# A running-sum copy moved ahead of the seventh exp, and another order of loading at the start

## The chip, the core and the metric

The kernel runs on one core of a Trainium2 chip. The metric is the device time of one execution in microseconds (us). Engines are named as the profile names them: PE is the matrix engine, PEld its weight loads, DVE the vector engine, ACT the scalar engine, POOL the GpSimd engine, SP the engine that issues most of the transfers. ACTq, SPq and DVEq mean that engine's sequencer (issue and waiting), not its arithmetic.

## The reference

Two graph layers, each with a residual and a layer norm, on x of 128 batches with 128 tokens and 512 features, all in float32, with an adjacency mask of 128 x 128 for each batch:

```python
# layer 0: masked attention with 8 heads of 64, then a projection
q, k, v = x @ Wq + bq, x @ Wk + bk, x @ Wv + bv
attn = softmax(where(adj > 0, q @ k.T / sqrt(64), -1e9))     # per head
x = layernorm(x + relu((attn @ v) @ Wo + bo))
# layer 1: additive attention over the same mask
Wh = x @ W
e = leaky(s_i[:, :, None] + s_j[:, None, :])       # s_i, s_j: Wh @ a1, Wh @ a2
att = softmax(where(adj > 0, e, -9e15), axis=1)
x = layernorm(x + leaky(att @ Wh))
```

## The kernel before

**Products with seven multiplications.** The five big products (x by Wq, Wk and Wv; the attention output by Wo; the layer-1 input by W) are cut into 2 x 2 blocks and done with seven block multiplications instead of eight (`strassen`, L279). Each product is a list of seven steps, called p1, p5, p6, p2, p7, p4, p3 in that order. Three of them, p1, p6 and p7, multiply into one running sum in PSUM, the bank that the trace calls `p_y` or `st_y`. After p1 and again after p6 and p7, ACT copies the running sum out to SBUF (`t0`, `t2`, `t3`), because the next step adds to the same bank and the intermediate sums are needed later. So the matrix engine may start p7 only once ACT has finished the copy `t2` that follows p6. The block sums of the left operand (`left_blocks`, L268) are four POOL operations; those of the weights (`right_blocks`, L134) are four DVE operations.

**Two kinds of product.** `group_product` (L328) makes q, k and v for four batches at a time (a group). Its steps are handed out through `group()` calls. `pair_product` (L413) does the projections by Wo and W for two batches at a time (a pair). Its steps are handed out through `pair()` calls. The copy of a pair's running sum is `read_out` (L434, the copy is line L436, tile `pr_t`). In odd stages the pair is a projection by Wo (`project_o`), in even stages one by W (`project_w`).

**The main loop** (L767) has one stage for each batch t. All five engines run in the order written there (`manual_schedule`), with waits only for data and buffers. In each stage after the third, the program starts the logits of batch t (L469), adds the mask, takes the maxima, runs eight exps on ACT, one for each head (L490), then eight divisions on ACT (L504), writes the result to DRAM and reads it back in another layout (`spread`, L508), and DVE transposes it in the next stage (`transpose`, L517). Between these calls stand `group()` and `pair()`. Before the change, p6 of the pair is the third `pair()` of the stage, and it stands after the seventh exp:

```python
            sm.exp(4, 5)
            last.transpose()
            group()
            sm.reciprocals(0)
            sm.exp(6)
            fin.store()
            pair()
            sm.exp(7)
```

On PE nothing stands between these lines but the multiplications of `group()` and `pair()`, and on DVE nothing of `pair()`. p7 follows at the next-but-one `pair()`.

**The start.** SP loads the four batches of the first group (`x_rows`), then half of Wq, Wk, Wv. ACT issues the other half of Wq and the two biases. DVE reorders the features of each batch (L733), PE transposes them (L743), DVE or ACT copies them to `xT` (L744). DVE scales four blocks of Wq (L747) and makes the block sums of Wq (L137 to L140). POOL makes the block sums of x (L273 to L276). For the first group the Q steps go p1, p2, p5, p6, p7. p1 and p2 use the first two batches and the first two blocks of Wq alone (XS[0], XS[1] and the ACT-issued half of Wq); p5 onward use the block sums. `x_turns` (L713) tells at which stage the later batches are transposed, and so when their loads (`xz`, L240, four for each batch) are issued. The block sums of Wv are written to DRAM (`wv`, L168) and fetched back piece by piece (`wv_n`, L386) through a ring of three buffers.

Of the kernel before, what the change touches and what calls it, by code (L numbers as in the profile page):

```python
# [17 lines left out]
GROUP = 4  # L18
# [6 lines left out]
def kernel(  # L25
# [56 lines left out]
    nc = tc.nc  # L82
    B, P, D = x.shape
# [179 lines left out]

    def sum_x(g):
        sums = big.tile([P, 3, 2, 2 * P], F32, name="xS")
        XS[g] = left_blocks(XT[g], sums)

    def left_blocks(xT, sums):  # L268


        xt = xT.rearrange("p (i c) (h t) -> p i h c t", i=2, h=2)
        a11, a12, a21, a22 = (xt[:, i, h] for h in range(2) for i in range(2))
        nc.gpsimd.tensor_add(sums[:, 0], a21, a22)  # L273
        nc.gpsimd.tensor_sub(sums[:, 1], sums[:, 0], a11)
        nc.gpsimd.tensor_sub(sums[:, 2], a11, a21)
        nc.gpsimd.tensor_sub(a21, a12, sums[:, 1])  # L276
        return (a11, a12, a21, a22, sums[:, 0], sums[:, 1], sums[:, 2])

    def strassen(bank, multiply, read, add):  # L279

# [86 lines left out]
    def products(g):  # L367

        for h in range(2):
            Q[g, h] = big.tile([P, NC, HALF], F32, name="qT", bufs=4)  # L370
            K[g, h] = big.tile([P, NC, HALF], F32, name="kT", bufs=3)
            V[g, h] = big.tile([P, 2, D], F32, name="v", bufs=3)

        def features_first(dst):
            return lambda h, o: dst[g, h][:, 2 * o : 2 * o + 2, :]

        def tokens_first(dst):
            return lambda h, o: dst[g, h][:, :, o * HALF : (o + 1) * HALF]

        ring, todo = {}, [0, 4, 5, 1, 6, 3, 2]  # L380

        def fetch():
            if todo:
                n = todo.pop(0)
                ring[n] = work.tile([P, 2, HALF], F32, name="wv_n", bufs=3)
                nc.sync.dma_start(ring[n], wv[n])  # L386

        chains = [
            group_product(g, 3 * g, lambda n: wq[:, PLACE[n]], features_first(Q), True, b_cols[:, 0, :]),
            group_product(g, 3 * g + 1, lambda n: wk[:, PLACE[n]], features_first(K), True),  # L390
            group_product(g, 3 * g + 2, ring.pop, tokens_first(V), False),
        ]

        def with_fetch(step, n=1):
            def run():
                step()
                for _ in range(n):
                    fetch()

            return run  # L400

        chains[1][0] = with_fetch(chains[1][0], 2)
        chains[2][0] = with_fetch(chains[2][0])
        chains[1][5] = with_fetch(chains[1][5])
        for n in (1, 2, 3):
            chains[2][n] = with_fetch(chains[2][n])

        order = [chains[0][n] for n in ((0, 3, 1, 2, 4) if g == 0 else range(5))]
        order += [chains[1][0], *chains[0][5:], *chains[1][1:5]]
        order += [chains[2][0], chains[1][6], chains[1][5], *chains[2][1:5]]  # L410
        return order + chains[2][5:]
# [112 lines left out]
    def attend(sm):  # L524

        b = sm.b
        v = V[b // GROUP, b % GROUP // 2][:, b % 2, :]
        p = psum("p_oT").rearrange("p (c q) -> p c q", c=NC)
        for c in range(NC):
            for r in range(2):  # L530
                h = 2 * c + r
                nc.tensor.matmul(  # L532
                    p[r * HD : (r + 1) * HD, c, :],
                    v[:, h * HD : (h + 1) * HD],
                    sm.paT[:, r * NC + c, :],
                    start=True,
                    stop=True,
                )
        pair, h = divmod(b, 2)

        def copy():
            if h == 0:
                OT[pair] = work.tile([P, NC, 2 * P], F32, name="oT")
            for c in range(NC):
                nc.scalar.activation(  # L545
                    OT[pair][:, c, h * P : (h + 1) * P],
                    p[:, c, :],
                    AF.Identity,
                    bias=b_cols[:, 1, c : c + 1],
                )  # L550
            if h == 1:
                sums = work.tile([P, 3, 2, P], F32, name="oS")
                OT[pair] = left_blocks(OT[pair], sums)

        return copy

# [56 lines left out]
    def transpose_x1(b):  # L613
        pair, h = divmod(b, 2)
        if h == 0:
            X1T[pair] = work.tile([P, NC, 2 * P], F32, name="x1T")
        transpose_blocks(X1T[pair][:, :, h * P : (h + 1) * P], X.pop((b, 1)))
        if h == 1:
            sums = work.tile([P, 3, 2, P], F32, name="x1S")
            X1T[pair] = left_blocks(X1T[pair], sums)  # L620

    def project_w(pair):

# [87 lines left out]
    sm = fin = edge = none  # L711

    def x_turns(t):  # L713
        if t < -1:
            return () if t == -3 else (4, 5, 6)
        return [b for b in [(), (t + 7, t + 8), (t + 8,), (t + 8,)][t % GROUP] if on(b)]

    x_rows = [work.tile([P, 2, D], F32, name="x_rows", tag=tag) for tag in ("pa", "paz")]  # L720
    for b in range(GROUP):
        nc.sync.dma_start(x_rows[b // 2][:, b % 2, :], x[b])
    load_blocks(Wq, columns(wq), nc.scalar, only=0)
    nc.scalar.dma_start(b_rows[:NC, :], bq.rearrange("(c p) -> c p", p=P))
    nc.scalar.dma_start(b_rows[NC:, :], bv.rearrange("(c p) -> c p", p=P))
    load_blocks(Wq, columns(wq), nc.sync, only=1)
    load_blocks(Wk, columns(wk), nc.sync)
    XT[0] = big.tile([P, NC, GROUP * P], F32, name="xT")
# [1 line left out]
    def order_features(b):  # L730
        rows = x_rows[b // 2][:, b % 2, :]
        turned = work.tile([P, D], F32, name="x_turned", tag="xz", bufs=3)
        nc.vector.tensor_copy(  # L733
            turned.rearrange("p (c q i) -> p c q i", q=4, c=4),
            rows.rearrange("p (q c i) -> p c q i", q=4, c=4),
        )
        return turned

    def transpose_rows(b, turned, copy):

        p = psum("p_x").rearrange("p (c k) -> p c k", c=NC)
        for c in range(NC):
            nc.tensor.transpose(p[:, c, :], turned[:, c * P : (c + 1) * P], ident)  # L743
        copy(XT[0][:, :, b * P : (b + 1) * P], p)  # L744
# [5 lines left out]
    turned = [order_features(b) for b in range(2)]  # L750
    transpose_rows(0, turned[0], nc.vector.tensor_copy)
    transpose_rows(1, turned[1], nc.scalar.copy)
    turned.append(order_features(2))
    scale(0)
    transpose_rows(2, turned[2], nc.scalar.copy)
    turned.append(order_features(3))
    scale(1)
    transpose_rows(3, turned[3], nc.vector.tensor_copy)
    turn_biases()
    sum_x(0)  # L760
    scale(2)
    wq_sums[0]()
    scale(3)
    for op in wq_sums[1:]:
        op()
    chores += right_blocks(places(wk)) + load_wv()
    for t in range(-3, B + 9):  # L767
        pair_steps = []
# [30 lines left out]
        if t < 3:  # L799
            sm.maxima()  # L800
            group(2)
            if on(t - 2):
                load_residual(t - 2)
            if t == 0 and on(GROUP):
                sum_x(1)
            sm.exp(0, 1, 2, 3)
            last.transpose()
            group()
            sm.reciprocals(0)
            sm.exp(4, 5, 6, 7)  # L810
            sm.reciprocals(1)
            sm.divide(0, 1, 2)
            group()
            copy_o = attend(last) if last is not none else none.copy
            sm.divide(3, 4)
            copy_o()
            sm.divide(5, 6, 7)
            if on(t + 1):
                mask_float(t + 1)
        else:  # L820
            sm.maxima()
            group()
            edge = EdgeSoftmax(t - 7) if on(t - 7) else none
            fin.residual()
            if on(t - 2):
                load_residual(t - 2)
            edge.maxima()
            fin.stats()
            if t % GROUP == 0 and on(t + GROUP):
                sum_x(t // GROUP + 1)  # L830
            pair()
            sm.exp(0, 1, 2, 3)
            edge.exp()
            pair()
            sm.exp(4, 5)
            last.transpose()
            group()
            sm.reciprocals(0)
            sm.exp(6)
            fin.store()  # L840
            pair()
            sm.exp(7)
            edge.divide()
            pair()
            sm.reciprocals(1)
            sm.divide(0, 1, 2, 3)
            group()
            sm.divide(4, 5)
            pair()
            sm.divide(6, 7)  # L850
            if on(t + 1):
                mask_float(t + 1)
            copy_o = attend(last) if last is not none else none.copy
            if t % 2 == 0:
                copy_o()
            group()
# [56 lines left out]
```

## Time and profile before

| | before |
|---|---|
| time, median of 3 (lowest to highest) | 2514.77 us (2514.57 to 2516.88) |
| span of the profiled execution | 2513.0 us |
| PE busy | 2444.2 us, 97% |
| PEld busy | 2000.3 us, 80% |
| DVE busy | 1817.5 us, 72% |
| ACT busy | 1429.8 us, 57% |
| POOL busy | 781.1 us, 31% |
| granted PE clock, mean | 0.989 |
| DMA | 379.92 MB, 151 GB/s |

A busy share is an average over the whole span. Where the span has stages with different limits, it says little about any one of them, so the views by stretch of time and the waits of single instructions have to be read beside it. In timeline rows the columns are start, busy time, engine, line, operation, tiles out<-in, shapes and count, and in brackets how long the engine had been idle and what released it.

### The profile page before, as it was taken

The numbers are of one execution on the slowest core, as the hardware profiler recorded it, in microseconds if no ns is written. First come the engines' busy times: TensorE is split into PE (matmuls) and PEld (weight loads), VectorE is DVE, ScalarE is ACT, GpSimd is POOL, SyncE is SP. The second block draws the span as 40 slices with busy tenths as digits, with TensorE's granted clock in tenths as the row PEclk, the third lists the DMA queues.
The fourth block names the chain that finished last, engine by engine and source line by source line (L and its number), as shares of the span: only waits on it lengthen the run. The fifth ranks groups of instructions, "written<-read, shape, count | busy, mean of one in ns | idle before, by whom it ended". The sixth has DMA issues, their size and how long they took to land.

```text
span 2513.0 us, 43768 instructions
## 1 busy us (share of the span) xinstructions
PE 2444.2 (97%) x13713; PEld 2000.3 (80%) x13713; DVE 1817.5 (72%) x3758; ACT 1429.8 (57%) x5187; POOL 781.1 (31%) x1161
## 2 busy tenths in 40 slices
PE   8899999999999999999999999999999999999975
PEld 6688888888888888888888888888888888888853
DVE  5767777777776777776777776777777777777675
ACT  2565565565565565565565556556556556556551
POOL 2222323322323323323323323323323323333232
PEclk9999999999999999999999999999999999999987
DMA  6544444544444544544544544544544444544531
GB/s 186 180 144 142 160 159 138 172 151 143 159 150 149 168 151 143 167 144 152 164 149 147 164 144 152 167 145 151 165 142 153 161 147 152 167 147 143 164 119 47
DMA packets 351112, 379.92 MB, mean 151 GB/s; under 512 B 38936, under 2 KB 255008, under 8 KB 350880
## 3 DMA queue, kind: packets, MB, share of 16 engines
q1 hardware_dynamic: 350288, 376.59, 46.6%
q8 instruction: 110, 1.80, 0.3%
q14 instruction: 122, 1.00, 0.1%
q10 hardware_dynamic: 592, 0.53, 0.1%
HBM read 240.91 MB, written 136.05 MB: 150 GB/s over the span
## 4 chain that ended last, share of the span: by engine, by line
PE 92%; DVE 3%; DMA 2%; ACT 1%; issue 1%; SPq 1%; POOL 0%; DVEq 0%; POOLq 0%; ACTq 0%
PE st_y L345 26%; PE p_y L425 17%; PE st_w L345 13%; PE p_w L425 8%; PE st_x L345 7%; PE lg L469 5%; PE p_oT L532 5%; PE p_h L672 4%; PE p_x L425 4%; ACT pa L490 1%; PE p_e L643 1%; PE p_e L644 1%; DMA wv_n<-wv 0%; ACT pa L504 0%; DVE st L559 0%
## 5 line engine op out<-in xcount | busy, mean ns | idle before, releaser
L564 POOL TENSOR_SCALAR ve<-mv 128x1 f32<-128x1 f32 x256 | 68.7, 268 | 1372.9 <-DVE mv L561 1372.9
L490 ACT ACTIVATE pa<-pa,nmax 128x128 f32<-128x128 f32 x1024 | 399.9, 392 | 48.3 <-DVE nmax L484 33.8
L504 ACT ACTIVATE pa<-pa,rs 128x128 f32<-128x128 f32 x1024 | 336.4, 395 | 30.1 <-DVE rs L500 30.1
L545 ACT ACTIVATE oT<-p_oT,b_cols 128x128 f32<-128x128 f32 x512 | 145.6, 367 | 202.1 <-PE p_w L425 200.1
L478 DVE TENSOR_TENSOR pa<-lg,mf 128x512 f32<-128x512 f32 x256 | 164.5, 684 | 100.6 <-PE lg L469 98.1
L322 ACT COPY st_t<-st_y 128x512 f32<-128x512 f32 x192 | 110.7, 577 | 157.1 <-PE st_y L345 157.1
L469 PEld LDWEIGHTS lg<-kT,qT 64*128 64x128 f32 x2048 | 124.2, 187 | 93.7 <-issue 93.7
L490 ACT ACTIVATION_READ_ACCUMULATOR pa<-pa,nmax 128x1 f32 x1024 | 193.3, 189 | 0.0
L566 POOL TENSOR_TENSOR rstd<-ve,mhalf 128x1 f32<-128x1 f32 x256 | 176.8, 691 | 21.4
L436 ACT COPY pr_t<-p_y 128x256 f32<-128x256 f32 (+1 forms) x384 | 139.7, 364 | 59.8 <-PE p_y L425 53.2
L519 DVE STREAM_TRANSPOSE paT<-paz 128x1024 f32<-128x1024 f32 x128 | 159.3, 1245 | 1.0 <-issue 0.3
L484 DVE TENSOR_REDUCE nmax<-pa 128x8 f32<-128x1024 f32 x128 | 156.2, 1220 | 4.4
L326 ACT ACTIVATE st_t<-st_y,b_cols 128x256 f32<-128x256 f32 x192 | 80.7, 471 | 126.2 <-PE st_y L345 126.2
L672 PE MATMUL p_h<-wh,att 128*128 128x512 f32 x256 | 133.9, 605 | 17.6 <-DVE att L663 17.6
L632 DVE TENSOR_TENSOR wh<-p_w,pr_t 128x257 f32<-128x257 f32 x128 | 54.1, 423 | 133.1 <-PE p_w L425 83.1
L425 PE MATMUL p_y<-w,x1S 128*128 128x257 f32 x512 | 136.5, 389 | 12.9 <-ACT pr_t L436 10.7
L469 PE MATMUL lg<-kT,qT 64*128 64x128 f32 x2048 | 148.7, 285 | 0.0
L532 PEld LDWEIGHTS p_oT<-paT,v 128*64 128x64 f32 x2048 | 111.0, 138 | 47.0 <-issue 41.2
L532 PE MATMUL p_oT<-paT,v 128*64 128x128 f32 x2048 | 142.3, 282 | 3.6 <-DVE paT L519 3.6
L425 PE MATMUL p_y<-wo,oS 128*128 128x256 f32 x512 | 132.6, 382 | 7.9 <-ACT pr_t L436 7.9
L646 ACT ACTIVATE e<-p_e,wh 128x128 f32<-128x128 f32 x128 | 47.3, 369 | 161.0 <-PE p_e L644 161.0
L425 PE MATMUL p_y<-w,x1T 128*128 128x257 f32 x512 | 135.4, 387 | 1.0 <-ACT pr_t L436 1.0
(151 smaller groups left out, 5958.9 us busy)
## 6 DMA issues: line engine op xcount, KB each, us to landing
pa_dram<-pa SPq DMA_DIRECT2D x128, 512.0 KB, 2.6
paz<-pa_dram SPq DMA_DIRECT2D x512, 128.0 KB, 2.6
wv_n<-wv SPq DMA_DIRECT2D x224, 256.0 KB, 2.9
x<-in_x_dram SPq DMA_DIRECT2D x128, 256.0 KB, 3.0
x_dram<-x SPq DMA_DIRECT2D x128, 256.0 KB, 2.3
xz<-x_dram SPq DMA_DIRECT2D x512, 64.0 KB, 2.0
out_dram<-z SPq DMA_DIRECT2D x128, 256.0 KB, 2.5
xz<-in_x_dram SPq DMA_DIRECT2D x496, 64.0 KB, 2.2
```

The lines of the kernel that those rows point to most:

```text
L345: nc.tensor.matmul(p[:, m, :], lhs, rhs, start=start and m == 0 and kc == 0, stop=True, skip_group_check=True,)
L425: nc.tensor.matmul(p[:, :width], xs[n][:, kc, :], w[:, PLACE[n], kc, :], start=start and kc == 0, stop=True, skip_group_check=True,)
L469: nc.tensor.matmul(self.lg[r][:, c, :], q[rows, c, cols], k[rows, c, cols], start=True, stop=True)
L478: nc.vector.tensor_add(by_head[:, r * NC : (r + 1) * NC], self.lg[r].rearrange("p c (b k) -> p c b k", b=4), mf.unsqueeze(1).to_broadcast( ...
L484: nc.vector.tensor_reduce(self.nmax, by_head, AX.XY, ALU.max, negate=True)
L490: nc.scalar.activation(self.pa[:, :, h, :], self.pa[:, :, h, :], AF.Exp, bias=self.nmax[:, h : h + 1], accum_out=self.sums[:, h : h + 1],)
L504: nc.scalar.activation(self.pa[:, :, h, :], self.pa[:, :, h, :], AF.Copy, scale=self.rs[:, h : h + 1])
L519: nc.vector.transpose(self.paT.rearrange("p h (a i) -> p a h i", i=32), self.paz.rearrange("p a (h k) -> p a h k", k=32),)
L532: nc.tensor.matmul(p[r * HD : (r + 1) * HD, c, :], v[:, h * HD : (h + 1) * HD], sm.paT[:, r * NC + c, :], start=True, stop=True,)
L545: nc.scalar.activation(OT[pair][:, c, h * P : (h + 1) * P], p[:, c, :], AF.Identity, bias=b_cols[:, 1, c : c + 1],)
L566: nc.gpsimd.tensor_tensor(rstd, ve, mhalf, ALU.pow)
L672: nc.tensor.matmul(p.rearrange("p (o f) -> p o f", o=2), edge.att, wh, start=True, stop=True)
```

## The change

It has two parts. The first moves the third `pair()` of each stage, p6 with its copy of the running sum, from behind the seventh exp to ahead of it, so that the copy comes earlier in ACT's order. The second reorders the start: x of batches 0 and 1 is loaded first on SP, the biases follow there, the first half of Wq and then x of batches 2 and 3 come on ACT; the first product stands ahead of the work on batches 2 and 3, which is put into a function that runs after p1; `left_blocks` returns its POOL operations instead of issuing them at once; both later copies of `xT` go to ACT; and loads of batches 5 and 6 move from before the Wv fetches to after them.

```diff
-        XS[g] = left_blocks(XT[g], sums)
+        XS[g], add = left_blocks(XT[g], sums)
+        return add
...
         order = [chains[0][n] for n in ((0, 3, 1, 2, 4) if g == 0 else range(5))]
+        if g == 0:
+            first = order[0]
+            order[0] = lambda: (first(), other_half())
...
-        if t < -1:
-            return () if t == -3 else (4, 5, 6)
+        if t < 0:
+            return {-3: (), -2: (4,), -1: (5, 6, 7)}[t]
...
-    for b in range(GROUP):
-        nc.sync.dma_start(x_rows[b // 2][:, b % 2, :], x[b])
+    for b in range(2):
+        nc.sync.dma_start(x_rows[0][:, b, :], x[b])
+    nc.sync.dma_start(b_rows[:NC, :], bq.rearrange("(c p) -> c p", p=P))
+    nc.sync.dma_start(b_rows[NC:, :], bv.rearrange("(c p) -> c p", p=P))
     load_blocks(Wq, columns(wq), nc.scalar, only=0)
-    nc.scalar.dma_start(b_rows[:NC, :], bq.rearrange("(c p) -> c p", p=P))
-    nc.scalar.dma_start(b_rows[NC:, :], bv.rearrange("(c p) -> c p", p=P))
+    for b in range(2):
+        nc.scalar.dma_start(x_rows[1][:, b, :], x[2 + b])
...
-    turned.append(order_features(2))
+    turn_biases()
     scale(0)
-    transpose_rows(2, turned[2], nc.scalar.copy)
-    turned.append(order_features(3))
     scale(1)
-    transpose_rows(3, turned[3], nc.vector.tensor_copy)
-    turn_biases()
-    sum_x(0)
-    scale(2)
-    wq_sums[0]()
-    scale(3)
-    for op in wq_sums[1:]:
-        op()
+    add_x = sum_x(0)
+    def other_half():
+        for b in (2, 3):
+            transpose_rows(b, order_features(b), nc.scalar.copy)
+        scale(2)
+        wq_sums[0]()
+        add_x()
+        scale(3)
+        for op in wq_sums[1:]:
+            op()
...
             sm.reciprocals(0)
+            pair()
             sm.exp(6)
             fin.store()
-            pair()
             sm.exp(7)
```

More of the change, by code (lines that the diff above doesn't have):

```diff
@@ L272, in left_blocks, with add @@
         a11, a12, a21, a22 = (xt[:, i, h] for h in range(2) for i in range(2))
[L273 to L277, printed above, removed]
+        def add():
+            nc.gpsimd.tensor_add(sums[:, 0], a21, a22)
+            nc.gpsimd.tensor_sub(sums[:, 1], sums[:, 0], a11)
+            nc.gpsimd.tensor_sub(sums[:, 2], a11, a21)
+            nc.gpsimd.tensor_sub(a21, a12, sums[:, 1])
+        return (a11, a12, a21, a22, sums[:, 0], sums[:, 1], sums[:, 2]), add
     def strassen(bank, multiply, read, add):
@@ L552, in copy @@
                 sums = work.tile([P, 3, 2, P], F32, name="oS")
-                OT[pair] = left_blocks(OT[pair], sums)
+                OT[pair], add = left_blocks(OT[pair], sums)
+                add()
         return copy
@@ L619, in transpose_x1 @@
             sums = work.tile([P, 3, 2, P], F32, name="x1S")
-            X1T[pair] = left_blocks(X1T[pair], sums)
+            X1T[pair], add = left_blocks(X1T[pair], sums)
+            add()
     def project_w(pair):
@@ L804 @@
             if t == 0 and on(GROUP):
-                sum_x(1)
+                sum_x(1)()
             sm.exp(0, 1, 2, 3)
@@ L829 @@
             if t % GROUP == 0 and on(t + GROUP):
-                sum_x(t // GROUP + 1)
+                sum_x(t // GROUP + 1)()
             pair()
```

## The prediction

> **What bounds the kernel now.** I read the busy time by stretch first, because 97% PE is an average. These rows give PE, PEld, DVE, ACT and POOL busy, then granted clock, DMA share and GB/s:
>
> ```profile
> 0.00:50.00 50.00, 39.21 (x177) 32.17 (x178) 27.70 (x40) 10.36 (x23) 12.90 (x17) 1.00 0.72 199
> 50.00:150.00 100.00, 89.06 (x514) 72.39 (x512) 68.34 (x148) 57.31 (x220) 19.41 (x24) 0.98 0.51 160
> 900.00:1200.00 300.00, 299.70 (x1703) 246.36 (x1701) 220.33 (x458) 176.76 (x646) 96.94 (x144) 1.00 0.48 153
> 2400.00:2513.00 113.00, 71.13 (x293) 49.20 (x291) 70.67 (x160) 36.13 (x124) 30.63 (x52) 0.76 0.26 89
> ```
>
> From 150 to about 2388 us PE is busy all but about 0.3 us in 300: a time saved there must come out of PE's own row. Idle PE lies at the two ends, 10.8 + 10.9 us in the first 150 and 42 us in the last 113.
>
> In the middle the chain of waits is PE alone, with one break that comes back. Two rows of PE, then the rows of ACT, around 1055 us:
>
> ```profile
> 1053.94 1.89 PE L345 MATMUL st_w<-xT,wq 128*128 128x256 f32 x8
> 1055.90 1.11 PE L425 MATMUL p_y<-w,x1S 128*128 128x257 f32 x4
> ...
> 1055.01 0.39 ACT L490 ACTIVATE pa<-pa,nmax 128x128 f32<-128x128 f32 x1
> 1055.31 0.19 ACT L490 ACTIVATION_READ_ACCUMULATOR pa<-pa,nmax 128x1 f32 x1
> 1055.40 0.36 ACT L436 COPY pr_t<-p_y 128x257 f32<-128x257 f32 x1
> 1055.65 0.41 ACT L490 ACTIVATE pa<-pa,nmax 128x128 f32<-128x128 f32 x1
> ```
>
> The first PE row is a group step (p3 of Q), the second is p7 of the pair. Matmuls of a stream follow 0.216 us apart; here the first of p7 starts 0.455 after its predecessor and the second 0.29 after that. p7's weight load begins at 1055.87, right after the copy L436 ended at 1055.76; in an undisturbed step it begins with the previous matmul. So this p7 loses (0.455 - 0.216) + (0.291 - 0.216) = **0.315 us** to a copy that ACT did behind the seventh exp (1055.01). Going through all starts of p7 and p6 in the trace, this happens once a group, at 149.2, 223.9 and on every 75.63 us to 2266.0, **29 times**. In the other three stages of a group p7 starts on time. Most of it stays hidden in busy time, since pipelined rows overlap.
>
> At the start, the rows that count are these (from the timeline, and the last two from the chain of waits):
>
> ```profile
> 10.49 0.43 DVE L747 TENSOR_SCALAR wq<-wq 128x512 f32<-128x512 f32 x1 [2.49 <-DMA wq<-in_L_gnn_Wq_dram]
> 12.55 3.51 PE L345 MATMUL st_y<-xT,wq 128*128 128x256 f32 x8
> 13.30 1.43 POOL L273 TENSOR_TENSOR xS<-xT 128x512 f32<-128x512 f32 x1 [11.40 <-DVE b_cols L115]
> 13.65 1.63 DVE L137 TENSOR_TENSOR wq<-wq 128x512 f32<-128x512 f32 x1
> 37.90 1.97 PE L345 MATMUL st_y<-wv_n,xT 128*128 128x256 f32 x8 [1.63 <-DMA wv_n<-wv]
> ...
> 34.60 4.27 DMA wv_n<-wv
> 40.32 6.15 DMA wv_n<-wv
> ```
>
> Wq lands at 10.46, the first product runs at 12.55; then PE waits for the first piece of Wv until 37.76, and the third piece lands at 46.47, just as PE needs it for p6 of V (46.52). From there to 114 us the chain runs through exps, DMA and DVE of the first softmaxes, so the landing at 46.47 sets when all that starts.
>
> **What the skill says.** The Trainium skill, "TensorE: Matmul & The Clock Gate", section "Step-by-step: what each phase is for": weight loads are pulled ahead of running matmuls. The trace agrees (load at 1037.16, its matmul at 1037.37, where nothing waits), and it is why a late copy costs more than its lateness at the matmul. The same page, "What's actually happening": the PE runs at half clock until about one 3.4 us window was busy, and the window runs freely. Here the clock record rises at 15.64 us, so the first product took 3.51 us against 1.89 warm. "SBUF — State Buffer", section "SBUF: two separate sides": a DVE operation with two SBUF inputs and a POOL operation exclude each other. Here L137 takes 1.63 us beside POOL, 0.68 alone (21.17 us). "DMA: Bandwidth & Descriptors", section "Issuing engines are not separate DMA queues": moving a load to another engine saves issue time only. In the trace ACT's and SP's loads land in the order of issue: x at 4.58, Wq at 4.83, 6.37, 7.80, x at 8.63.
>
> **Part 1: p6 ahead of the seventh exp.** It adds and removes nothing; neither PE's nor DVE's order changes. On ACT the copy comes ahead of one exp, which takes 0.39 us from start to start (1055.01 to 1055.40). At the 29 stalls the running sum has long been ready (p6's matmuls end by 1053.3) and the exp starts at 1055.01, so the copy would end at about 1055.37 instead of 1055.76. p7's weight load would want to begin at 1055.45, about 0.11 us after a copy's end: 1055.48. What is left of the stall is about 0.03 us. Gain 29 x (0.315 - 0.03) = **8.3 us**; bounds: 29 x 0.315 = 9.1, and 6.5 if some 0.09 is left each time.
>
> What queues behind the copy: the seventh and eighth exps, the divisions, the write to DRAM. In three of four stages ACT finds the running sum finished, so the sum of its work to the eighth exp is the same. In the fourth (1034 us) p6 ends at 1034.95, after the sixth exp at 1034.39, and ACT would sit idle 0.56 us; the later work slips by 0.39. It is caught up at once: the next ACT row waits for PE until 1037.58, and the divisions ahead of it would end at 1037.3. Cost 0.
>
> In the last stages with a softmax PE waits for the same copy much longer: 4.99 us at 2411.61 and 3.26 at 2426.65, and there the chain goes exps, copy, p7. One exp less ahead of it: 2 x 0.39 = **0.8 us**. At 2396.25 the chain goes on through ACT's divisions: 0.
>
> **Part 2: the start.** Bytes are the same, so by order of issue the first half of Wq has 0.5 MB of x less ahead of it. Its fourth piece reuses the completion semaphore of the first x and so is issued at that landing, 4.6; it should land near 8.1 (0.9 MB ahead of it end near 7.0, then one piece of the other half and itself, 0.6 us each as in the landings from 9.26 to 9.89). ACT's copy of batch 1 stands behind the issue of x 2 and 3 (each waits for an earlier landing, 6.4 and about 7.1) and the table load of 1.28: near 9.3. The first product then starts at about 9.4, 3.1 us earlier. It doesn't keep that: still at half clock it takes about 3.5 us, and now the two transposes for batches 2 and 3 (1.1 us each cold) come behind it. So p2 starts near 15 instead of 15.7, p7 of Q is 0.5 to 1.5 us earlier.
>
> What decides is the chain to the third Wv piece: Wv's block sums on DVE (23.8), write (24.5), 30 issues on SP at 0.43 to 0.48 us each without a break, landing 46.47. Its length stays; its start moves. DVE does three sums of Wq before POOL starts, but the later ones and Wk's two beside it: I work out Wk's end at about 22.2 instead of 23.9, bounded below by Wv's landing at 20.84. So the chain starts **1.5 us** earlier, between 0.3 and 3. The first Wv pieces now go out eight issues (3.5 us) sooner, so the wait of 1.63 at 37.90 vanishes; that only makes PE wait later, at V's p6. The third DVE transpose moved before the first mask add (0.6 us each) fits in DVE's 1.39 us idle at 44.44: 0. Past 46 us everything is relative to this point.
>
> Sum: 8.3 + 0.8 + 1.5 = 10.6; 2514.8 - 10.6 = **2504.2 us**.
>
> **Rivals.** (a) The wait moves: with p7 early PE runs on into another copy or into the transposed softmax, and gets only half of part 1. Against it: the transpose that p_oT needs ends at 1055.16, well before 1056.6. Then 2514.8 - 4 - 1.5 = 2509. (b) The start keeps its whole 3.1 us, and the half-clock spell at 114.6 us (3.4 us long, 1.3 lost: 3.22 for a step of 1.89) goes too: 2514.8 - 9.1 - 0.8 - 3.1 - 1.3 = 2500.5. For it: PE's idle 2.55 us before 114.07 may fall otherwise; against it the DVE and SP chain. (c) Slower: ACT's 0.39 slip in the fourth kind of stage reaches PE through the write and the transpose: 30 x 0.39 = 11.7 lost, nothing else gained but the stalls, 2514.8 + 11.7 - 8.3 = 2518. Against it: the catch-up above.
>
> **How the numbers follow.** Forecast 0.70, (a) 0.12, (b) 0.13, (c) 0.05. The range from 2500.3 to 2508.8 takes in (b), the bounds 6.5 and 0.3 of the unknown costs, and nearly (a). Faster by over 5 us means under 2509.7: the forecast, (b) and nearly all of (a), 0.92; within 0.2% 0.05; slower 0.03.
>
> **What would show it.** The p7 behind p3 of Q at 0.22 instead of 0.455 from its predecessor, and 75.3 instead of 75.6 us between groups; the first product near 9.4 us; no wait for Wv near 36; V's p6 near 45. It would be wrong if a new PE wait came once a group, if Wq landed no sooner, or if the first softmax started later than 49.1.

## The result, and the profile after

| | before | after |
|---|---|---|
| time, median (lowest to highest) | 2514.74 us (2514.57 to 2516.88), 4 runs | 2503.16 us (2501.05 to 2505.38), 4 runs |
| span of the profiled execution | 2513.0 us | 2502.1 us |
| PE busy | 2444.2 us | 2438.1 us |
| granted PE clock, mean | 0.989 | 0.989 |

After takes 0.9952 of the time of before (95% interval 0.9935 to 0.9969), 11.6 us less by the medians and 10.9 by the profiled spans. The forecast was 2504.2.

The same views as before, first the busy time by stretch (PE, PEld, DVE, ACT, POOL, then clock, DMA share, GB/s):

```profile
0.00:50.00 50.00, 39.82 (x185) 32.83 (x185) 29.35 (x43) 13.56 (x37) 12.81 (x17) 1.00 0.77 208
50.00:150.00 100.00, 89.73 (x503) 73.12 (x504) 65.01 (x144) 54.18 (x205) 18.26 (x24) 0.95 0.51 154
900.00:1200.00 300.00, 300.00 (x1708) 248.18 (x1707) 221.51 (x457) 177.30 (x645) 96.77 (x144) 1.00 0.48 154
2400.00:2502.00 102.00, 62.06 (x254) 43.00 (x254) 63.84 (x148) 33.24 (x117) 28.68 (x48) 0.79 0.24 82
```

In the middle PE is busy all of 300 us and does 1708 matmuls where it did 1703. In the second row the clock is 0.95 where it was 0.98, and PE gets through 503 matmuls where it got through 514: there the start's gain is lost again, as shown below.

The stall in the middle, in PE's rows and then in ACT's rows of the same stage:

```profile
1050.61 1.89 PE L349 MATMUL st_w<-xT,wq 128*128 128x256 f32 x8
1052.33 1.03 PE L432 MATMUL p_y<-w,x1S 128*128 128x257 f32 x4
```

```profile
1050.96 0.81 ACT L330 ACTIVATE qT<-st_y,b_cols 128x256 f32<-128x256 f32 x2
1051.68 0.36 ACT L443 COPY pr_t<-p_y 128x257 f32<-128x257 f32 x1
1051.93 0.41 ACT L497 ACTIVATE pa<-pa,nmax 128x128 f32<-128x128 f32 x1
```

The copy now stands ahead of the seventh exp and ends at 1052.04, before the last matmul of p3 of Q starts (1050.61 + 7 x 0.216 = 1052.12). p7 starts 1.72 us after that step's start, eight matmuls of 0.216, where it took 1.96, and its four rows take 1.03 where they took 1.11. Over the trace the step into p7 is 0.216 us in all 30 groups; there is no stall left.

The start, from the timeline:

```profile
7.67 0.76 DVE L758 TENSOR_SCALAR wq<-wq 128x512 f32<-128x512 f32 x2
8.72 3.40 PE L349 MATMUL st_y<-xT,wq 128*128 128x256 f32 x8 [1.28 <-DMA x_rows<-in_x_dram]
14.04 1.26 POOL L276 TENSOR_TENSOR xS<-xT 128x512 f32<-128x512 f32 x1 [12.14 <-ACT xT L755]
15.36 2.00 PE L349 MATMUL st_w<-xS,wq 128*128 128x256 f32 x8 [0.64 <-POOL xS L276]
33.94 1.89 PE L349 MATMUL st_y<-wv_n,xT 128*128 128x256 f32 x8
43.77 2.00 PE L349 MATMUL st_y<-wv_n,xS 128*128 128x256 f32 x8 [1.47 <-DMA wv_n<-wv]
46.33 0.40 ACT L497 ACTIVATE pa<-pa,nmax 128x128 f32<-128x128 f32 x1
```

The first product starts 3.83 us earlier, V's first step has no wait, the third piece of Wv is waited for as before but lands earlier, and the first exp starts at 46.33 instead of 49.08. These are the signs that the prediction named; the first product and V's p6 come even earlier than it said.

**Where the gain arises.** I took one landmark, the start of the logits of a batch on PE, and subtracted its time after from its time before:

| up to | before - after | what lies in between |
|---|---|---|
| logits of batch 1 to 4 | +2.7 to +3.0 us | the start |
| logits of batch 5 | -0.45 | stage 4, which gives all of it back |
| logits of batch 125 | +8.66 | 29 stalls: +9.11, or 0.314 each |
| end | +10.8 | the last stages: +2.15 |

Stage 4 is the surprise. The chain of waits there, and PE's rows:

```profile
108.95 2.63 DMA wv_n<-wv
```

```profile
111.72 3.75 PE L349 MATMUL st_y<-wv_n,xS 128*128 128x256 f32 x8 [2.96 <-DMA wv_n<-wv]
116.14 3.78 PE L349 MATMUL st_y<-wv_n,xT 128*128 128x256 f32 x8 [0.67 <-ACT st_t L326]
119.72 2.44 PE L349 MATMUL st_w<-wv_n,xT 128*128 128x256 f32 x8
```

A step of eight matmuls takes 1.89 us at full clock. Here two take twice as long and a third 2.44: the clock record of this profile is at half from 110.6 to 120.8 us. Before had such a spell too, 3.4 us from 114.6, and there one step is hit:

```profile
114.07 3.22 PE L345 MATMUL st_y<-wv_n,xS 128*128 128x256 f32 x8 [2.55 <-ACT pa L504]
```

### The profile page after: what moved, and what is told of

The parts are those of the page before. It is cut to its first block, busy times and chain, and to the rows that moved or that the text cites. A ratio compares the mean times of both kernels' runs of the same rounds, so it can differ in the third digit from the quotient of the medians.

```text
span 2502.1 us, 43770 instructions
## 1 busy us (share of the span) xinstructions
PE 2438.1 (97%) x13713; PEld 2006.4 (80%) x13713; DVE 1815.5 (73%) x3757; ACT 1429.1 (57%) x5188; POOL 779.0 (31%) x1161
## 4 chain that ended last, share of the span: by engine, by line
PE 93%; DVE 2%; issue 1%; ACT 1%; DMA 1%; POOL 1%; SPq 0%; POOLq 0%; DVEq 0%; ACTq 0%
PE st_y L349 26%; PE p_y L432 17%; PE st_w L349 13%; PE p_w L432 9%; PE st_x L349 7%; PE lg L476 5%; PE p_oT L539 5%; PE p_h L681 4%; PE p_x L432 4%; PE p_e L653 1%; PE p_e L652 1%; DMA wv_n<-wv 1%; ACT pa L497 0%; DVE st L567 0%; ACT pa L511 0%
## 5 line engine op out<-in xcount | busy, mean ns | idle before, releaser
L326 ACT COPY st_t<-st_y 128x512 f32<-128x512 f32 x192 | 110.6, 576 | 157.4 <-PE st_y L349 157.4
L574 POOL TENSOR_TENSOR rstd<-ve,mhalf 128x1 f32<-128x1 f32 x256 | 176.5, 690 | 21.3
```

Source lines behind the costliest of these rows:

```text
L574: nc.gpsimd.tensor_tensor(rstd, ve, mhalf, ALU.pow)
```

## The experiments

One theory and its rivals. **A:** the stalls give their 9 us because the copy no longer stands behind an exp; the start gains about 3 us by where the loads stand; and stage 4 gives back more or less of it by the half-clock spell, which is no part of the change but of where an idle stretch of PE falls. **Its rivals:** the gain of the middle comes with the new start rather than with the copy (B); the new order of work on PE and DVE, not the loads, makes the early start; or the copy, moved early, costs the softmax something that only the sum hides (C). The letters in an expectation are those of its own run. Ratios are to before, on the same chip, with 95% intervals. Profiles are of single executions.

**The copy alone** (before, with part 1 of the change).

```diff
             sm.reciprocals(0)
+            pair()
             sm.exp(6)
             fin.store()
-            pair()
             sm.exp(7)
```

> The kernel before with only p6 of the pair moved ahead of the seventh exp; the start is as before. Theory A (the repeated copy stall is most of the gain): 29 stalls x 0.315 us = 9.1, and up to 0.8 in the last stages, so about 2504.9 us; the step from p3 of Q to p7 of the pair falls from 0.455 to 0.216 us and groups come every 75.3 us. Rival B (the start carries the change): 2 us or less, above 2512.

Measured: 2503.95 us against 2514.58, ratio 0.9955 (0.9943 to 0.9967). The step into p7 is 0.216 in all 30 groups. By the landmarks it stands at -1.32 at batch 5 and at +7.79 at batch 125, so the middle gains 9.1 us. The copy alone carries nearly the whole gain.

**The start alone** (after, with p6 back behind the seventh exp).

```diff
             sm.reciprocals(0)
-            pair()
             sm.exp(6)
             fin.store()
+            pair()
             sm.exp(7)
```

> The changed kernel with p6 back behind the seventh exp, so only the start is changed. Theory A (the start wins about 2.75 us by 99 us and gives it back to a half-clock spell of PE at 110 us): 2512 to 2516 us, with the 29 stalls of 0.315 us back; logits of batch 4 near 99.3 us instead of 102.2, logits of batch 5 not earlier than 121. Rival B (the start carries its gain to the end): 2512.0 or less in every run.

Measured: 2513.27 us, ratio 0.9992 (0.9984 to 1.0). The 29 stalls are back (0.443). V's p6 starts at 44.88, the landmark of batch 1 at +1.64, that of batch 5 at -0.20: stage 4 has a half-clock spell of 6.8 us. By the medians the start is worth about 1 us of the time, and the interval reaches 1.0, so it can't be told from nothing; in this profile its early gain is there and lost.

**The copy one exp later** (before, with p6 behind the eighth exp): a dose of the suspected cause.

```diff
             sm.exp(6)
             fin.store()
-            pair()
             sm.exp(7)
+            pair()
```

> The kernel before with p6 of the pair moved the other way, behind the eighth exp. Theory A (p7 waits for ACT's copy, and each exp ahead of it costs 0.39 us there): 29 x 0.39 = 11.3 us more stall, about 0.8 more in the last stages, so about 2526.9 us; the step into p7 grows from 0.455 to about 0.85 us, in one stage of four only. Rival B (something else sets p7): 2514.7, no change.

Measured: 2525.55 us, ratio 1.0043 (1.0031 to 1.0055), about what one further exp of delay for each group gives: the period of a group grows by 0.375 us. The rows of PE in the stage that is hit, then those of ACT:

```profile
1059.32 1.89 PE L345 MATMUL st_w<-xT,wq 128*128 128x256 f32 x8
1061.66 1.11 PE L425 MATMUL p_y<-w,x1S 128*128 128x257 f32 x4 [0.45 <-ACT pr_t L436]
```

```profile
1060.77 0.39 ACT L490 ACTIVATE pa<-pa,nmax 128x128 f32<-128x128 f32 x1
1061.16 0.36 ACT L436 COPY pr_t<-p_y 128x257 f32<-128x257 f32 x1
```

The step into p7 is now 0.829 us (0.455 before, 0.216 after), still in one stage of the four only, and only now does PE's row show an idle time (0.45). With the two runs above, the stall follows the place of the copy by one exp for each step.

**A fill for the idle stretch of stage 4** (after, with 22 transposes of the identity on PE ahead of V's p7; their results are never read).

```diff
             copy_o = attend(last) if last is not none else none.copy
+            if t == 4:
+                fill(22)    # nc.tensor.transpose(p[:, :P], ident, ident), 22 times
             if t % 2 == 0:
```

> The changed kernel with 22 extra transposes of the identity on PE in stage 4, between the attention product of batch 3 and p7 of V (their result is never read). They should take about 2.4 us of the 2.96 us in which PE idles there. Theory A (the idle stretch drops the PE clock to half, and that costs the start's gain): no half-clock spell near 110 us; p7, p4 and p3 of V take 1.9 us each instead of 3.75, 3.78 and 2.44, so about 4 us less than the profiled run of the changed kernel, near 2499.7, and less scatter from run to run. Rival B (the loss near 110 us is a wait for data, not the clock): no gain, 2503 or more.

Measured: 2499.82 us, ratio 0.9938 (0.9925 to 0.9951), 3.3 us under after's median. PE's rows:

```profile
110.12 2.62 PE L715 MATMUL p_f<-ident 128*128 128x128 f32 x22
113.12 1.96 PE L349 MATMUL st_y<-wv_n,xS 128*128 128x256 f32 x8 [0.38 <-DMA wv_n<-wv]
115.76 1.99 PE L349 MATMUL st_y<-wv_n,xT 128*128 128x256 f32 x8 [0.68 <-ACT st_t L326]
```

The wait for the Wv piece is the same, since the fill and the 0.38 left of it take its place; but no half-clock spell follows, and V's p7 and p4 take 1.96 and 1.99 us where they took 3.75 and 3.78. Stage 4, from the logits of batch 4 to those of batch 5, takes 18.23 us instead of 22.82. This one profile doesn't show that the fill did it: a kernel without a fill (the copy four places earlier, below) has no spell here either, and both have one of 3.4 us near 80.7 us instead, ahead of stage 4. What speaks for the fill is its five times, 2498.84 to 2501.45 us, against 2501.00 to 2505.38 in the nine of after; as ratios to before, 0.9938 against 0.9952 and 0.9951.

**Loads of batches 5 and 6 back ahead of the Wv fetches** (after, otherwise).

```diff
-            return {-3: (), -2: (4,), -1: (5, 6, 7)}[t]
+            return {-3: (), -2: (4, 5, 6), -1: (7,)}[t]
```

> The changed kernel with the later batches of x loaded as before: batches 4, 5 and 6 ahead of the first fetches of Wv, 7 behind. Theory A (the third Wv piece decides, and it stands at the same place of SP's order either way): PE waits 1 to 2 us for the first Wv piece again (V's p1 near 35.5 us instead of 34), but V's p6 starts where it does in the changed kernel, 43.8 to 44.9 us, and the total stays within 1.5 us of it, 2502 to 2505. Rival B (the earlier fetches carry the start's gain): V's p6 near 46.5 and 2505 or more.

```profile
36.49 1.97 PE L349 MATMUL st_y<-wv_n,xT 128*128 128x256 f32 x8 [1.86 <-DMA wv_n<-wv]
45.01 1.99 PE L349 MATMUL st_y<-wv_n,xS 128*128 128x256 f32 x8
```

Measured: 2504.40 us, ratio 0.9952 (0.9938 to 0.9966), the same as after. The wait for the first Wv piece comes back (1.86 us), the one for the third goes, and V's p6 starts 1.24 us later than after's, 0.1 past the expected range. This part moves a wait; the time can't tell it from nothing.

**The old loads with the new order of work** (after, with x on SP and the biases on ACT as before).

```diff
-    for b in range(2):
-        nc.sync.dma_start(x_rows[0][:, b, :], x[b])
-    nc.sync.dma_start(b_rows[:NC, :], bq.rearrange("(c p) -> c p", p=P))
-    nc.sync.dma_start(b_rows[NC:, :], bv.rearrange("(c p) -> c p", p=P))
+    for b in range(GROUP):
+        nc.sync.dma_start(x_rows[b // 2][:, b % 2, :], x[b])
...
     load_blocks(Wq, columns(wq), nc.scalar, only=0)
-    for b in range(2):
-        nc.scalar.dma_start(x_rows[1][:, b, :], x[2 + b])
+    nc.scalar.dma_start(b_rows[:NC, :], bq.rearrange("(c p) -> c p", p=P))
+    nc.scalar.dma_start(b_rows[NC:, :], bv.rearrange("(c p) -> c p", p=P))
```

> The changed kernel with the loads of x, Wq and the biases in the old order; the order of the work (first product ahead of batches 2 and 3, POOL's sums late) stays new. Theory A (DVE gains because it does most of its sums of Wq before POOL starts): the first product starts near 11.5 to 12.5 us, yet DVE reaches Wv's sums near 22.8 to 23.3 instead of 23.8 of before, and V's p6 starts near 45.5. Rival B (all comes from the earlier Wq): DVE reaches Wv's sums at 23.8 or later and V's p6 starts at 46.5 or later. In time the two differ by about 1 us, so the landmarks of the trace decide.

Measured: 2505.49 us, ratio 0.9954 (0.9942 to 0.9967). Rival B of its expectation met the landmarks and theory A missed them: the first product is back at 12.55, and V's p6 comes at 47.87, later than before's 46.52. DVE's and POOL's rows:

```profile
19.68 0.69 DVE L367 TENSOR_TENSOR qT<-st_x,st_t 128x512 f32<-128x512 f32 x1 [2.77 <-PE st_x L349]
20.29 1.42 DVE L137 TENSOR_TENSOR wk<-wk 128x512 f32<-128x512 f32 x1
21.75 1.64 DVE L138 TENSOR_TENSOR wk<-wk 128x512 f32<-128x512 f32 x1
25.58 0.68 DVE L137 TENSOR_TENSOR wv_t<-wv_t 128x512 f32<-128x512 f32 x1
```

```profile
18.55 1.26 POOL L276 TENSOR_TENSOR xS<-xT 128x512 f32<-128x512 f32 x1 [16.65 <-ACT xT L753]
```

With the transposes of batches 2 and 3 behind p1, POOL's sums start at 18.55 (13.30 before) and DVE waits 2.77 us for PE's p2; then Wk's sums fall beside POOL's work and take 1.42 to 1.64 us instead of 0.68. Wv's sums start at 25.58 (23.82 before). In this profile the new order of work by itself costs 1.4 us up to the logits of batch 1, part of it by the clock, which rises at 17.54 us here and at 15.64 in before. So the gain needs the earlier loads. The earlier loads with the old order of work were not run, so it isn't shown how much they bring alone.

**The copy four places earlier** (after, with p6 and the group step ahead of the fifth exp).

```diff
             pair()
-            sm.exp(4, 5)
             last.transpose()
             group()
             sm.reciprocals(0)
             pair()
+            sm.exp(4, 5)
             sm.exp(6)
```

> The changed kernel with p6 of the pair ahead of the fifth exp too, so that ACT, which reaches the copy earlier, waits for PE in more stages and runs its last four exps and the divisions later (by about 1.6 us in one stage of four). Theory A (the stall is gone already and ACT's later work has slack): no further gain and no loss, 2502 to 2505. Rival C (of the prediction: ACT's lateness reaches PE through the write and the transpose): 30 x about 1 us slower, 2530 or more.

Measured: 2498.47 us, ratio 0.9929 (0.9916 to 0.9941). No further gain was expected and some 5 us came. The middle is unchanged (+9.10 from batch 5 to batch 125), as it must be with no stall left. The last stages gain 5.40 instead of 2.15. There the copy is on the path. PE's row of p7 in stage 126, in after and then in this kernel:

```profile
2403.54 2.05 PE L432 MATMUL p_y<-w,x1S 128*128 128x257 f32 x4 [4.61 <-ACT pr_t L443]
```

```profile
2399.57 2.05 PE L432 MATMUL p_y<-w,x1S 128*128 128x257 f32 x4 [3.84 <-ACT pr_t L443]
```

It waits 0.77 less, two exps of 0.39. The rest of the gain isn't traced: in the last stages the clock is at half for 42.2 us here and for 48.6 in after, which is a part of it. This profile also has no half-clock spell near 110 us; whether the edit or chance removed it stays open. A loss from moving the copy far ahead (rival C) isn't there: ACT has the slack.

**Fills in all idle stretches** (after, with 12 transposes in stage 2, 22 in stage 4, and 22 to 44 at seven places in the last stages; results never read).

```diff
+            if t in TAIL:        # 126: 36, 127: 22, 128: 22, 130: 22
+                fill(TAIL[t], True)
...
+        if t in TAIL_H:          # 131: 44, 133: 40, 134: 40
+            fill(TAIL_H[t], True)
```

> The changed kernel with extra transposes of the identity (results never read) in PE's longest waits: 12 in stage 2 and 22 in stage 4 ahead of and behind the attention products, 36, 22, 22 and 22 ahead of p7 in stages 126, 127, 128 and 130, and 44, 40 and 40 ahead of the last layer-1 products in stages 131, 133 and 134. Theory A (half-clock spells after waits cost time also in the last 115 us: p7 2.05 instead of 1.03 us, attention product 1.87 instead of 1.09, last products 2.09 instead of 1.02 three times): about 6 us less than with stage 4 alone filled, near 2494. Rival B (the last stages are bound by DVE and ACT, PE's clock is beside the point, or the extra work delays PE): 2499 or more.

Measured: 2497.89 us, ratio 0.9928 (0.9915 to 0.994): less than expected. The last stages gain 9.2 us by the landmarks, and the mean clock is 0.997: the half-clock spells between 2384 and 2480 us, 27 us of after's profile, are all gone. But the profile shows spells of 3.4 us at 46.0 and 110.8 us, ahead of and in the very stage that was filled, and stands at -1.35 at batch 5. So a fill of fixed length at a fixed place doesn't rule a spell out. Here PE had waited one step ahead of the fill, 3.27 us for p2's piece of Wv (0.56 to 1.99 in the eleven profiles without a fill in stage 2; whether that fill makes this wait longer wasn't tried). That a fill makes a spell in stage 4 rarer rests on the times of the fill in stage 4 alone.

**After and before once more**, for the scatter.

> The changed kernel once more, for a second profile and more times. Theory A (the length of the half-clock spell near 110 us changes from run to run with the position of the clock's window): the 29 stalls are gone again, the first product is near 8.7 us and V's p6 at 43.8 to 45 us, but the spell has another length or place (3.4 or 6.8 us, or near 80 us), and times spread over 3 us or more around 2503. Rival B (the spell belongs to the program): 10.2 us near 110 again, and times within 1 us.

> The kernel before once more, for a second profile of its start. Theory A: 29 stalls of 0.315 us at the same steps, V's p6 between 46 and 48.5 us, a half-clock spell near 111 us of 3.4 or 6.8 us. Rival B (the spell belongs to the program): 3.4 us at 114.6 us again, all landmarks within 0.1 us.

After: 2502.28 us, ratio 0.9951 (0.9938 to 0.9963). Its profile has a spell of only 3.4 us in stage 4 where the first had 10.2. Its landmarks stand at +3.26 at batch 1, +2.58 at batch 5, +11.69 at batch 125 and +13.8 at the end: the same kernel, and the start's gain kept. The same stretch of stage 4 in the two profiles of after, in that of the fill in stage 4, and in that of the copy four places earlier, which has no fill (clock is the third column from the right):

```profile
100.00:125.00 25.00, 19.77 (x96) 15.15 (x95) 13.98 (x29) 8.38 (x32) 12.46 (x15) 0.80 0.64 194
```

```profile
100.00:125.00 25.00, 20.02 (x105) 15.87 (x104) 16.95 (x30) 10.48 (x40) 12.93 (x15) 0.93 0.63 191
```

```profile
100.00:125.00 25.00, 22.83 (x146) 18.54 (x145) 18.69 (x34) 11.03 (x40) 14.31 (x16) 1.00 0.62 188
```

```profile
100.00:125.00 25.00, 20.40 (x125) 16.32 (x124) 19.06 (x36) 11.26 (x41) 14.49 (x16) 1.00 0.62 189
```

Clock 0.80, 0.93, 1.00 and 1.00, and 96, 105, 146 (22 of them the fill) and 125 matmuls done in the same 25 us. So the same program loses or keeps its start's gain with the length of the spell. Before once more (one run, 2518.0 us): landmarks within some 0.3 us of the first profile at the start, stalls of 0.451, and a spell at the same place (114.5) and of the same length. That fits the rival of its expectation, a spell that belongs to the program; but the kernel with the copy alone moved, which has the same start, has one of 6.8 us at 114.8.

**The best version** (the copy four places earlier, with the fills, two of them shorter).

> p6 of the pair ahead of the fifth exp, and the extra transposes in PE's longest waits (12 in stage 2, 22 in stage 4, 28, 12, 22 and 22 ahead of p7 in stages 126, 127, 128 and 130, 44, 40 and 40 ahead of the last layer-1 products). Theory A (two gains in the last stages that add: fewer exps ahead of the copy for which p7 waits, and a full PE clock): about 3 us below either alone, near 2495, where the two alone had 2498.5 and 2497.9. Rival B (both shorten the same wait): 2497.5 or more.

Measured: 2495.64 us, ratio 0.9923 (0.9909 to 0.9937): it beats both kernels. The two gains add only in part. From the logits of batch 125 to the end this profile takes 114.9 us, where after takes 122.6, the earlier copy 119.4 and the fills 115.6; a full sum would be 112.3. Against either alone (ratios 0.9929 and 0.9928) the intervals overlap. PE's waits for the copy over the whole span, in after and in this kernel (us in total, times, longest):

```profile
PE p_y L432 <- ACT pr_t L443: 18.5, 10, 4.6
```

```profile
PE p_y L432 <- ACT pr_t L443: 12.0, 14, 1.7
```

The fills stand in some of these waits, so they look shorter by the fill as well as by the copy's new place.

And the last stages, after and this kernel:

```profile
2380.00:2480.00 100.00, 73.95 (x346) 53.78 (x342) 69.67 (x156) 41.18 (x149) 29.51 (x49) 0.86 0.29 98
```

```profile
2380.00:2480.00 100.00, 84.61 (x522) 66.71 (x521) 74.08 (x167) 41.56 (x152) 29.90 (x50) 1.00 0.29 99
```

The clock is whole where it was 0.86. What PE does more in this stretch is the fill itself, 189 transposes; the work behind it runs at full clock.

## Why the prediction was right, step by step

The time and the main cause held; the split of the smaller terms didn't, and the total is nearer than its parts. The terms, one by one:

- **Part 1, the stalls.** 8.3 forecast, 9.11 measured, the upper bound. The copy came where the forecast put it, 1.43 us after the start of p3 (1052.04 - 1050.61; 1055.37 - 1053.94 forecast). The weight load too: it begins at 1052.15, 0.11 after the copy's end and 0.03 after the last matmul's start (1052.12), as forecast. What failed is the step from there to the residue of 0.03 on PE: p7's first matmul still starts on time, 0.216 after its predecessor, so a load that is late by this much costs nothing. The count (29) and the size (0.315; 0.314 measured) held. That an edit of one line of order could be priced to 0.01 us came from reading the step between matmul starts, since PE's idle column showed nothing.
- **ACT's slip in the fourth kind of stage.** 0 forecast and 0 measured: 29 steps of 0.315 are the whole difference in the middle. Rival (c) falls with it, and once more with the copy moved four places.
- **Rival (a), a new wait in the middle.** None appeared; PE is busy 300.00 of 300.
- **The last stages.** 0.8 forecast, 2.15 measured. The two waits did what was forecast: at the named p7 they fell from 4.99 to 4.61 and from 3.26 to 2.88, together 0.76. The other 1.4 us was no part of the sum. Some of it is the clock: before's p7 at 2463.66 took 2.05 us, the same step of after 1.11 (2454.36), and in the last stages the clock is at half for 55.4 us in before and 48.6 in after. Nor can the whole be put down to the copy: the stretch from the logits of batch 125 to the end takes 124.8 and 127.0 us in the two profiles of before, 123.5 with the start alone changed, 123.3 with the copy one exp later, and 122.6 to 123.2 in six profiles with the copy ahead of the seventh exp. So the 2.15 is no more than the two profiles of before differ by, and only the 0.76 is read from its waits.
- **Part 2, up to 46 us.** 1.5 forecast, 2.7 to 3.0 measured in this profile, 1.5 to 3.3 by the logits of batch 1 in five others with the same start and loads, so inside the stated 0.3 to 3 or just above; in a sixth, with a half-clock spell at 46.0 us, 0.35. Two terms were mis-sized. The transposes of batches 2 and 3 took 1.04 us for both (11.95), not 1.1 each, so p2 of Q kept most of the lead (12.83 against 15.89). That is in part luck: the clock had risen at 11.60; with the start alone changed it rose at 14.68, and they took 1.92. And Wv came earlier too (the sixth of its eight pieces landed at 19.11, in before at 19.80), so the lower bound taken from before moved as well; Wv's sums start at 21.41, 2.4 earlier, where 1.7 was forecast. The chain from there to V's p6 kept its length, as said: 22.36 us after (21.41 to 43.77), 22.70 before.
- **The wait for Wv.** It vanished at V's p1, as forecast, and PE waits 1.47 for the third piece instead.
- **"Past 46 us everything is relative."** This step failed. Stage 4 took 22.82 us against 19.40, so the start's gain was gone by batch 5. Rival (b) had the half-clock spell as something that could go; I didn't ask whether it could grow. The Trainium skill, "TensorE: Matmul & The Clock Gate", section "What's actually happening", says that the clock falls after an idle window of about 3.4 us, that the window runs freely, and that the number of slow matmuls changes from run to run for that reason. The traces agree on the length and on the change: the spells last 3.4, 6.8 or 10.2 us, and the same kernel had one of 10.2 and one of 3.4. They differ on the idle window: in the 3.41 us before after's fall at 110.58, PE was still busy for 1.16.

So the forecast came within 1.1 us of the measured median partly by luck, because errors cancel: +0.8 on the stalls, +1.4 on the last stages, +1.5 on the start (3.0 by batch 4), and -3.4 in stage 4. An estimate: with the 18.0 to 18.2 us that stage 4 takes in profiles without a spell there, instead of 22.82, the profiled run of 2503.92 would stand near 2499.

Where an idle stretch falls among the windows decides in large part whether a spell follows. With the copy one exp later PE idled 2.79 us before V's p7 and no spell came: an edge of the windows, counted on in steps of 3.41 us from the changes in the clock record, cut the stretch at 114.25, and PE was busy for 2.05 and 1.42 us of the two windows. I cut all 13 profiles into such windows, up to 160 us and from 2370 us on. The clock fell after each of the 79 windows at full clock in which PE was busy for less than 0.42 of the time, and after none of the 794 with more than 0.48; of the 25 between, it fell after 8. By this measure the fill of stage 4 lifted the two windows that it touches to 0.85 and 0.89; without it they would be at about 0.54 and 0.45 (an estimate, its own time taken off), so in that profile a spell might have stayed away anyway.

What stays open: what exactly decides whether a spell near 110 us lasts one, two or three windows. A window at half clock that was busy for 0.80 ended the spell in before (114.63) and didn't in after (113.99). The wait of 2.96 us for a Wv piece, issued at 108.95 and landed at 111.58, is the idle stretch that the spell follows in after. An earlier issue of that piece was not tried.

## What to carry to other kernels

A short copy that another engine waits for belongs ahead of long work in the copying engine's order even where the waiting engine shows no idle time: look at the step between starts of its pipelined rows, multiply by how often it comes back, and test the reading by moving the copy the other way as well. A gain at the start of a kernel is not safe until the next idle stretch of PE has passed, so compare landmarks along the span and the granted clock, not ends alone. Where PE must idle for some 3 us, a fill of cheap matmuls (here transposes) can keep the clock up, as it did in the last stages, and it delays nothing if it ends before the wait does; take several runs to judge it, since one profile can lack a spell by chance.

## What the runs showed of the hardware

- Half-clock spells in the middle of the span come in lengths of 3.4, 6.8 and 10.2 us. Stage 4 took 18.04, 18.10 and 18.23 us in the three profiles without one, 19.4 to 20.1 in four with 3.4 us near its usual place, 21.2 to 21.4 in three with 6.8, and 22.8 with 10.2. Two filled kernels with 3.4 us took 21.3 and 21.7: in both PE first waited over 3 us one step ahead of the fill, and in the best version V's p7 starts at 114.61 right behind the fill, with no wait left, so there the fill itself may cost time:

```profile
107.57 3.51 PE L349 MATMUL st_x<-wv_n,xT 128*128 128x256 f32 x8 [3.66 <-DMA wv_n<-wv]
112.15 2.62 PE L718 MATMUL p_f<-ident 128*128 128x128 f32 x22
```

- The weight load that waits for a copy begins 0.11 us after the copy's end (medians of 0.113, 0.114 and 0.115 in before, after and with the copy one exp later). A copy that ends 0.08 us ahead of the start of the last matmul before p7 costs nothing; one that ends 0.31 us behind it costs 0.315 us of PE, while the row shows at most 0.1 us of idle time. 0.37 later still, it costs 0.375 more, and the idle time then shows as 0.45.
- 22 transposes of the 128 x 128 identity in a row take 2.62 us on PE, 0.119 us each, at full clock. In the last stages such fills left no half-clock spell between 2384 and 2480 us, in two kernels of two.
